# Flamingo cross-attention block with a long convolution: half-size transforms on half-reversed tokens, and a searched instruction order

## The chip, the cores and the metric

The kernel runs on one core of one Trainium2 chip. The metric is the device time of one launch in microseconds (us), from three runs of the kernel; a profiled execution, taken separately, gives the trace. Five engines with strict in-order queues share the work: PE (TensorE, matmuls), DVE (VectorE), ACT (ScalarE), POOL (GpSimd) and SP (SyncE, which issues most DMAs).

## The reference

The input is `x` of 8 batches x 512 tokens x 256 channels and a context of 8 x 1024 x 192, all float32. Per batch:

```
Q = ln(x) @ Wq ; K = ctx @ Wk                 # 4 heads of 32
scores = Q K^T / sqrt(32) ; keep the 32 largest of 1024 per row ; softmax over them
c = mean over heads of (probs @ ctx) @ Wv
h = ln(ln(x)) * (1 + g*scale_in(c)) + g*shift_in(c)
y = causal convolution of h along the 512 tokens with a kernel K[256, 512] + h * D_skip
y = y * (1 + g*scale_out(c)) + g*shift_out(c)
t = ln(x) + y ; t = t + gelu(ln(t) @ W1 + b1) @ W2 + b2
x = x + tanh(g1) * ln(t)
x = x + tanh(g2) * (shared_swiglu(ln(x)) + the one of 8 expert swiglus that the gate picks)
```

The convolution's kernel is computed on the chip from the state-space parameters (`A`, `C`, `log_dt`), once.

## The kernel before, in words

**Tiles.** Tokens lie on the 128 partitions, in NT = 4 blocks of 128 per batch; channels (256) lie along the free dimension. Everything is float32; a float32 matmul leaves two records in the trace.

**Stages of a batch.** `prepare` loads `xt` and `cx`, normalises, transposes (`pc`, `px`) and makes `kT`, `qT` (`pk`, `pq`). `attention` makes the scores of two heads at a time in `scores`: four 32-row matmuls `pS` into two PSUM banks (tag `sc`), which ACT copies to `sc` and DVE reads once more in `mn`; DVE's MAX8 and MATCH_REPLACE8 then find the 32nd largest value; ACT exponentiates; POOL adds the heads into `acc`; `weighted` transposes `acc` (`pa`) and multiplies it with the context (`pu`). `mixed` modulates (`film`: `pfi`, then `pfo`) and convolves. `after_mix` is the MLP (`hT`, `pm`, `am`), two layer norms, the gate, the scatter of the tokens by expert into the DRAM table `xtab`, and the shared expert (`p1`, `p2`, shown as `p`, and `ae`). `block` and `routed` gather 128 tokens of one expert from `xtab` (`xb`, `pxb`), load that expert's three weight matrices of 512 KB (`rt_gate`, `rt_up`, `rt_down`) and run it (`pg`, `pu`, `pyr`), then scatter-add into the output.

**The convolution before.** The 512 tokens are two halves of L = 256 (the axis `b` of 2 in the rearrangements), each of NL = 2 blocks `c` of 128. `spectrum` multiplies both halves at once (512 columns) with cosine and sine tables `ftab`: two groups of 128 frequencies `f`, real and imaginary part `r`, two blocks `c`, so 8 matmuls of 128x512 into `pxf`. DVE and POOL multiply with the kernel's spectra `kf` (`yf`, `t2`, `t3`). The way back is 8 more, `py`, two outputs of four terms.

**The order of the work.** The program first writes down every operation (class `Plan`) with its inputs, its outputs, a planned cost (`time`) and a priority `k`: the place at which it was written down, less a lead (`LEAD_A`, `LEAD_P`, `LEAD_S`). `order` then walks through a model of the five engines, the pools and the DMA wire: at each step, of the operations that could begin first, it takes the one with the smallest `k` (on ACT, one that needs another activation table counts as 100 later). The order so found is issued, and each engine executes its own part strictly in it. All operations are issued from line 323, `o.fn()`, so the profile's rows tell them apart by tile names. The order of batches is fixed: attention of batch b runs beside `mixed` and `after_mix` of batch b-1 and the routed blocks of batch b-2; 15 routed blocks are left for the end.

Of the kernel before, what the change touches and what calls it, by code (L numbers as in the profile page):

```python
# [22 lines left out]
P = 128  # L23
# [17 lines left out]

HOP = {"PE": 0.28, "DVE": 0.15, "ACT": 0.22, "POOL": 0.18, "SP": 0.1, "DMA": 0.1}
# [3 lines left out]
class Op:  # L46
    __slots__ = ("i", "eng", "fn", "cost", "lat", "table", "acc", "succ", "npred", "est", "tiles", "end", "start", "what", "k")


class Plan:  # L50
    def __init__(self, nc):
        self.nc = nc
        self.ops = []
        self.noting = False
        self.lead = 0
        self.seen = {}
        self.tiles = {}
        self.queues = {}
# [78 lines left out]
    def time(self, eng, method, out, outs, ins, args, kw, n):  # L137
# [7 lines left out]
        if eng == "DVE":  # L145
            width = max([n] + [self.width(v) for v in ins])
            if method in ("max", "match_replace", "tensor_reduce", "bn_stats", "bn_aggr", "reciprocal", "max_index"):
                t = 0.065 + 0.0012 * width
                if method in ("match_replace", "max_index"):
                    t += 0.08  # L150
            elif method in ("tensor_scalar", "tensor_copy", "memset"):
                t = (0.09 + 0.00115 * width) if psum else (0.30 + 0.0006 * width)
            elif len(outs) > 1:
                t = 0.25 + 0.00133 * width
            else:
                t = 0.07 + 0.0012 * width + (0.0 if psum else 0.1 + 0.0008 * width)
            return t, None
        if eng == "ACT":
            t = max(0.24, 0.085 + 0.00104 * n) + (0.19 if len(outs) > 1 else 0)
            if not psum and 128 < n <= 256:  # L160
                t += 0.16
            f = args[2] if method == "activation" else None
            return t, (TABLES.get(str(f).split(".")[-1]) if f is not None else None)
        if eng == "POOL":
            if kw.get("op") == ALU.pow or (len(args) > 3 and args[3] == ALU.pow):
                return 1.05, None
            if method in ("memset", "iota"):
                return 0.3 + 0.0005 * n, None
            if method in ("tensor_scalar", "tensor_copy"):
                return 0.23 + 0.002 * n, None  # L170
            return 0.17 + (0.0028 if out.dtype == I32 and method == "tensor_tensor" and args[3] == ALU.add else 0.0022) * n, None
# [9 lines left out]
    def add(self, op, ins, outs, whole=False):  # L181
        op.i = len(self.ops)
        op.k = op.i - self.lead
# [36 lines left out]
    def order(self):  # L220

        ops = self.ops
        free = {e: 0.0 for e in ("PE", "DVE", "ACT", "POOL", "SP")}
        table = None
        wire = 0.0
        left = {t: len(v[1]) for t, v in self.tiles.items()}
        last = {t: 0.0 for t in self.tiles}
        slots = {}
        for q in self.queues.values():
            slots[id(q)] = [0.0] * q[0]  # L230
        granted = set()
        avail = {e: [] for e in free}
        done = []

        def offer(op):
            op.npred -= 1
            if op.npred == 0:
                avail[op.eng].append(op)

        for op in ops:  # L240
            op.npred += 1 + len(op.tiles)

        def grant(q):
            s = slots[id(q)]
            while s and q[2] < len(q[1]):
                t = q[1][q[2]]
                q[2] += 1
                at = min(s)
                s.remove(at)
                for i in self.tiles[t][1]:  # L250
                    ops[i].est = max(ops[i].est, at)
                    offer(ops[i])

        for q in self.queues.values():
            grant(q)
        for op in ops:
            offer(op)
        total = len(ops)
        while len(done) < total:
            best = None  # L260
            for e, a in avail.items():
                if not a:
                    continue
                t = free[e]
                first = min(max(t, o.est) for o in a)
                c = None
                for o in a:
                    if o.est <= first:
                        k = o.k + (SWITCH if e == "ACT" and o.table not in (None, table) else 0)
                        if c is None or k < c[0]:  # L270
                            c = (k, o)
                o = c[1]
                st = max(t, o.est)
                if best is None or (st, o.k) < best[0]:
                    best = ((st, o.k), o, st)
            assert best is not None, "nothing can begin"
            _, o, st = best
            e = o.eng
            avail[e].remove(o)
            cost = o.cost  # L280
            if e == "ACT" and o.table not in (None, table):
                cost += 1.3
                table = o.table
            o.start = st
            free[e] = o.end = st + cost
            done.append(o)
            if o.lat is not None:
                wire = max(o.end, wire) + (o.lat - 2.9 if o.lat > 2.9 else 0.0)
                fin = max(o.end + o.lat, wire + 2.9)
                o.end = fin  # L290
            else:
                fin = o.end
            for i in o.succ:
                s = ops[i]
                hop = HOP["DMA" if o.lat is not None else e] if (s.eng != e or o.lat is not None) else 0.0
                s.est = max(s.est, fin + hop)
                offer(s)
            for t in o.tiles:
                left[t] -= 1
                last[t] = max(last[t], fin)  # L300
                if left[t] == 0:
                    q = self.tiles[t][0]
                    slots[id(q)].append(last[t] + 0.15)
                    grant(q)
        self.total = max(o.end for o in ops)
        self.free = free
        return done

    def ahead(self, gen, lead):
        while True:  # L310
            self.lead = lead
            end = next(gen, StopIteration) is StopIteration
            self.lead = 0
# [12 lines left out]
SLOW = 1.05  # L326
# [17 lines left out]
def tile_kernel(ctx: ExitStack, tc: tile.TileContext, a: dict, out: bass.AP):  # L344
# [10 lines left out]
    ND, NH, NIC, NF = D // P, HID // P, NI // P, T // P  # L355

# [45 lines left out]
    def accs(name):  # L402
# [14 lines left out]
                     base=0, channel_multiplier=-1)  # L417
    plan.noting = True
# [12 lines left out]
    def prepare(b, s):  # L431
# [46 lines left out]
        for c in range(ND):  # L478
            p_ = bank(f"px{b}_{c}")
            for t in range(NT):  # L480
                TE.transpose(p_[:, t * P : (t + 1) * P], s.xt[:, t, c * P : (c + 1) * P], ident)
            S.copy(xT[:, c, :], p_)
        yield
        s.qT = pk.tile([P, T], F32, tag="qT", name=f"qT{b}")
# [20 lines left out]
    for b, s_ in enumerate(states):  # L505
        s_.prep = plan.ahead(prepare(b, s_), LEAD_P)
# [15 lines left out]
    ftab = const.tile([P, 3, NL, L], F32, name="ftab")  # L522
# [58 lines left out]
    def transposed(src, tag, name, g=None, b=None):  # L581

        t_ = pr.tile([P, ND, T], F32, tag=tag, name=name)
        for c in range(ND):
            p_ = bank(f"{name}_p{c}")
            for t in range(NT):
                TE.transpose(p_[:, t * P : (t + 1) * P], src[:, t, c * P : (c + 1) * P], ident)
# [5 lines left out]

    def spectrum(src, f, r, name):

        p_ = bank(name)
        blocks = src.rearrange("p (b c) d -> p c b d", b=2)
        for c in range(NL):
            TE.matmul(p_, ftab[:, r, c, f * P : (f + 1) * P], blocks[:, c],
                      start=(c == 0), stop=(c == NL - 1))  # L600
        return p_.rearrange("p (b d) -> p b d", b=2)


    def setup():
# [179 lines left out]
        q.dma_start(gin[:, 1], row(a["L0_xattn_b_norm_in"], DK + 1))  # L784
        ft = a["ftab"].rearrange("(c p two) r f -> p two r c f", p=P, two=2)
        for i, r in enumerate((0, 1, 1)):
            SY.dma_start(ftab[:, i], ft[:, 0, r, :NL, :L])
        altc = a["alt"].rearrange("(p o) -> p o", o=1)
        altr = a["alt"].rearrange("(o p) -> o p", o=1)
        for c in range(NL):  # L790
            SY.dma_start(ftab[:, 1, c, 0:1], altc)
# [690 lines left out]
```

## Time and profile before

| | us |
|---|---|
| median of 3 runs | 1792.97 (1792.47 to 1794.63) |
| profiled execution | 1794.11 |
| its span (first to last instruction) | 1792.3 |
| busy PE | 1513.1 (84%) |
| busy DVE | 1302.1 (73%) |
| busy ACT | 1154.6 (64%) |
| busy POOL | 931.5 (52%) |
| mean granted PE clock | 0.874 of full speed |

"Busy" is time in which an engine executes at least one instruction. A row of a group reads: line, engine, operation, output tile<-input tiles, shapes, number of records; then busy time, mean of one record in ns; then the time that the engine had stood idle just before them, and what ended it. Matmul records overlap, so their mean is longer than their share of the time.

### The profile page before, as it was taken

The page shows a single profiled execution, that of the slowest core. Times are in us where ns is not written, and L with a number is a line of the kernel's source. Part 1 is how long each engine was busy: PE and PEld are TensorE (multiplying, and loading weights), DVE is VectorE, ACT ScalarE, POOL GpSimd, SP SyncE. Part 2 cuts the span into 40 slices and gives each one's busy share as a digit, 9 for nine tenths or more (in the row PEclk, how much of TensorE's full clock was granted, in tenths as well). Part 3 has the DMA queues.
Part 4 walks back from the last instruction along what each step waited for, and adds up shares of the span by engine and source line. Part 5 has one row for each costly group of instructions (what it writes and reads, how often), then busy time and mean ns, then how long its engine had stood idle before and what let it go on. Part 6 is the DMA issues. An engine that isn't in the chain of part 4 may idle for free. (4 is left out here: it accounts for less than half of the span.)

```text
span 1792.3 us, 21191 instructions
## 1 busy us (share of the span) xinstructions
PE 1513.1 (84%) x6363; PEld 893.1 (50%) x6363; DVE 1302.1 (73%) x3073; ACT 1154.6 (64%) x2008; POOL 931.5 (52%) x1072
## 2 busy tenths in 40 slices
PE   5365577797998798999889999998999989889885
PEld 2143333344543454465436554654465547547685
DVE  6989977885878697977798889697978987222210
ACT  4778844676747774887578877885788678123121
POOL 5578544445363645465555765474557646233122
PEclk8555677786998799998989999998999989989898
DMA  4000110001200120143103330431033205523794
GB/s 118 0 1 24 33 35 18 12 12 47 70 20 12 47 65 18 36 128 96 54 12 109 91 102 12 135 107 58 12 111 107 66 12 162 179 103 86 228 280 117
DMA packets 101289, 131.68 MB, mean 73 GB/s; under 512 B 9687, under 2 KB 73004, under 8 KB 101166
## 3 DMA queue, kind: packets, MB, share of 16 engines
q1 hardware_dynamic: 93102, 121.05, 21.1%
q0 software_dynamic: 7008, 8.42, 2.6%
q8 instruction: 52, 0.85, 0.2%
q10 hardware_dynamic: 1056, 0.79, 0.1%
q14 instruction: 71, 0.58, 0.1%
HBM read 112.22 MB, written 18.78 MB: 73 GB/s over the span
## 5 line engine op out<-in xcount | busy, mean ns | idle before, releaser
L323 PE MATMUL pS<-kT,qT 32*128 32x512 f32 x512 | 285.6, 742 | 71.2 <-DVE mn L323 61.0
L323 POOL TENSOR_TENSOR acc<-acc,e 128x1024 f32<-128x1024 f32 x96 | 229.0, 2385 | 182.3 <-ACT e L323 179.9
L323 DVE MAX8 top<-mn 128x8 f32<-128x256 f32 (+1 forms) x512 | 276.0, 556 | 11.9
L323 ACT COPY sc<-pS 128x512 f32<-128x512 f32 x256 | 145.6, 584 | 167.1 <-PE pS L323 136.9
L323 DVE SCALAR_TENSOR_TENSOR e<-sc,t,e 128x1024 f32<-128x1024 f32 x128 | 180.3, 1421 | 40.6 <-ACT e L323 40.3
L323 DVE TENSOR_TENSOR mn<-sc,pS 128x512 f32<-128x512 f32 x256 | 165.2, 677 | 35.9 <-PE pS L323 19.9
L323 POOL TENSOR_TENSOR mn<-mn 128x256 int32<-128x256 int32 x128 | 102.4, 800 | 164.4 <-DVE hi L323 163.8
L323 PEld LDWEIGHTS pS<-kT,qT 32*128 32x128 f32 x512 | 75.9, 208 | 203.6 <-DVE mn L323 98.9
L323 ACT ACTIVATE e<-sc,sm 128x1024 f32<-128x1024 f32 x128 | 145.1, 1146 | 16.1 <-POOL acc L323 13.2
L323 ACT ACT_TABLE_LOAD x118 | 151.4, 1283 | 4.0 <-issue 2.0
L323 PE MATMUL pm<-hT,w 128*128 128x512 f32 x256 | 137.9, 677 | 13.6 <-ACT hT L323 13.6
L323 ACT ACTIVATE junk<-sc,sm 128x1024 bf16<-128x1024 f32 x128 | 146.1, 1141 | 1.3
L323 PEld LDWEIGHTS pu<-aT,cx 128*96 128x96 f32 x1024 | 122.2, 168 | 28.6 <-issue 24.1
L323 PE MATMUL pu<-aT,cx 128*96 128x128 f32 x1024 | 135.4, 282 | 0.2 <-ACT aT L323 0.2
L323 PE MATMUL am<-w,ga 128*128 128x256 f32 x512 | 129.1, 398 | 6.1 <-ACT ga L323 6.1
L323 PEld LDWEIGHTS am<-w,ga 128*128 128x128 f32 x512 | 96.9, 196 | 51.4 <-issue 27.6
L323 POOL DMA_INDIRECT out_dram<-yb,to x38 | 61.5, 1620 | 96.7 <-DMA out_dram<-yb,to 46.3
L323 ACT ACTIVATE e<-e,sm 128x1024 f32<-128x1024 f32 x96 | 108.5, 1147 | 1.6 <-DVE sm L323 1.6
L323 POOL TENSOR_TENSOR mn<-mn,hi 128x256 int32<-128x256 int32 x128 | 104.9, 819 | 8.0
L323 DVE TENSOR_TENSOR ger<-sgr,pu 128x512 f32<-128x512 f32 x38 | 26.0, 684 | 108.7 <-PE pu L323 105.9
L323 DVE MATCH_REPLACE8 mn<-top,mn 128x256 f32<-128x256 f32 x256 | 104.6, 409 | 0.0
L323 POOL TENSOR_TENSOR yf<-yf,t 128x512 f32<-128x512 f32 (+1 forms) x80 | 85.2, 1089 | 35.0 <-DVE t L323 33.7
(287 smaller groups left out, 3125.0 us busy)
## 6 DMA issues: line engine op xcount, KB each, us to landing
rt_gate<-in_L_ffn_rt_gate_dram SPq DMA_DIRECT2D x38, 512.0 KB
rt_up<-in_L_ffn_rt_up_dram SPq DMA_DIRECT2D x38, 512.0 KB
rt_down<-in_L_ffn_rt_down_dram SPq DMA_DIRECT2D x38, 512.0 KB
w<-in_L_xattn_W_dram SPq DMA_DIRECT2D x32, 512.0 KB
cx<-in_ctx_dram SPq DMA_DIRECT2D x7, 768.0 KB
xtab<-zt SPq DMA_DIRECT2D x8, 642.5 KB
xb<-xtab SPq DMA_DIRECT2D x38, 128.5 KB
xt<-in_x_dram SPq DMA_DIRECT2D x8, 512.0 KB
```

The lines of the kernel that those rows point to most:

```text
L323: o.fn()
```

## The change

Four things change together.

1. *Tokens.* Of each pair of 128-token blocks (t = 0,1 and t = 2,3), the odd block is kept in reverse order from `prepare` to `after_mix`. `anti` is the exchange matrix. Odd blocks are transposed with it instead of `ident`, so that `qT` is in reverse order and `hT` back in natural order. A matmul with `anti` turns the odd blocks of `xt` (and two columns of statistics) into reverse order; ACT copies them back. In the MLP two matmuls with `anti` add the odd blocks of `xr` in natural order into the accumulators `am`, so that ACT only copies these out.
2. *Transforms.* With tokens n and 255-n of a half on the same partition, frequencies of even and odd number need only their sum or only their difference. DVE makes the difference `df` and, in place, the sum; each of four spectra is then one matmul instead of two. Back, the even and the odd part (`pyu`, `pyw`) are two outputs of two terms each, and their sum and difference are the two blocks. The frequencies of a group are now all even or all odd; the tables are cut in set-up from `ktab` and `htab`.
3. *Planned costs.* The formulas of `time` have other constants (`SLOW` 1.05 becomes 1.12).
4. *The order.* `walk` is the same model as before, written with heaps. `order` tries 220 sets of shifts of the priorities, by kind of work (attention, preparation, scores, routed blocks, the rest) and sixteenth of the program, and keeps the set with the shortest sum of two walks in which every cost is drawn up to 20% longer.

```diff
-                    t = 0.065 + 0.0012 * width
+                    t = 0.15 + 0.00104 * width
...
+    def order(self):
+        self.compile()
+        rng = random.Random(1)
+        ops = self.ops
+        part = [(o.kind, o.i * PARTS // len(ops)) for o in ops]
+        longer = [[o.cost * (1.0 + SPREAD * rng.random()) for o in ops] for _ in range(2)]
+        def tried(shift):
+            _, done = self.walk([o.k - shift[p] for o, p in zip(ops, part)])
+            return sum(self.walk(order=done, cost=c)[0] for c in longer), done
+        shift = dict.fromkeys(part, 0)
+        parts = list(shift)
+        best, order = tried(shift)
+        for _ in range(WALKS):
+            new = dict(shift)
+            for p in rng.sample(parts, rng.choice((1, 2, 4, 8))):
+                new[p] += rng.choice((-1, 1)) * rng.choice((10, 30, 80, 200))
+            t, o = tried(new)
+            if t <= best:
+                best, order, shift = t, o, new
...
-SLOW = 1.05
+WALKS, PARTS, SPREAD = 220, 16, 0.2
+SLOW = 1.12
...
+    turn = (ident, anti)
...
-                TE.transpose(p_[:, t * P : (t + 1) * P], s.xt[:, t, c * P : (c + 1) * P], ident)
+                TE.transpose(p_[:, t * P : (t + 1) * P], s.xt[:, t, c * P : (c + 1) * P], turn[t % 2])
...
+        for v, n in ((s.xt, D), (s.rs2.unsqueeze(2), 1)):
+            p_ = bank(f"pr{b}_{n}")[:, : 2 * n].rearrange("p (b d) -> p b d", b=2)
+            x1 = v.rearrange("p (b c) d -> p c b d", c=2)[:, 1]
+            TE.matmul(p_, anti, x1, start=True, stop=True)
+            S.copy(x1, p_)
...
+        xs, xd = (xm.rearrange("p (b c) d -> p c b d", c=2)[:, k] for k in range(2))
+        df = pk.tile([P, 2, D], F32, tag="sg", name=f"df{b}")
+        V.tensor_sub(df, xs, xd)
+        V.tensor_add(xs, xs, xd)
...
-            re, im = (spectrum(xm, f, r, f"pxf{b}_{f}_{r}") for r in range(2))
+            re, im = bank(f"pxf{b}_{f}_0"), bank(f"pxf{b}_{f}_1")
+            for r, p_ in enumerate((re, im)):
+                TE.matmul(p_, ftab[:, r, f], xs if f == r else df, start=True, stop=True)
...
-        for c in range(NL):
-            p_ = bank(f"py{b}_{c}")
-            steps = [(f, r) for f in range(NL) for r in range(2)]
-            for i, (f, r) in enumerate(steps):
-                TE.matmul(p_, ftab[:, 2 * r, f, c * P : (c + 1) * P], yf[:, f, r].rearrange("p b d -> p (b d)"),
-                          start=(i == 0), stop=(i == len(steps) - 1))
...
+        pu, pw = bank(f"pyu{b}"), bank(f"pyw{b}")
+        for p_, k in ((pu, 0), (pw, 1)):
+            for f in range(NL):
+                r = f if k == 0 else 1 - f
+                TE.matmul(p_, itab[:, f, r], yf[:, f, r].rearrange("p b d -> p (b d)"),
+                          start=(f == 0), stop=(f == NL - 1))
+        x0, x1 = (xr.rearrange("p (b c) d -> p c b d", c=2)[:, k] for k in range(2))
+        pw3 = pw.rearrange("p (b d) -> p b d", b=2)
+        S.copy(x0, pu.rearrange("p (b d) -> p b d", b=2))
+        V.tensor_sub(x1, x0, pw3)
+        V.tensor_add(x0, x0, pw3)
...
+            if k == 0:
+                for t in range(1, NT, 2):
+                    TE.matmul(acc[t // 2][:, 1, :], anti, xr[:, t, :], start=False, stop=False,
+                              skip_group_check=True)
...
-            V.tensor_add(xr[:, 2 * i : 2 * i + 2], xr[:, 2 * i : 2 * i + 2], acc[i])
+            V.tensor_add(xr[:, 2 * i], xr[:, 2 * i], acc[i][:, 0])
+            S.copy(xr[:, 2 * i + 1], acc[i][:, 1])
```

## The prediction

> **What bounds the kernel now.** I read first the busy time by stretch. The stretches end where the last score matmul of batch 0 ends (233.6 us), where that of batch 7 ends (1484.3), where the last attention sums are reduced (1550.5) and where the last scatter of tokens has landed (1680.6). Columns: length, then busy us and instructions of PE, weight loads, DVE, ACT, POOL, then granted clock, DMA share, GB/s.
>
> ```profile
> 0.00:233.60 233.60, 125.73 (x757) 71.44 (x757) 197.01 (x336) 170.15 (x288) 151.75 (x142) 0.61 0.15 40
> 233.60:1484.30 1250.70, 1126.77 (x4178) 622.17 (x4177) 1024.74 (x2519) 889.84 (x1549) 676.67 (x797) 0.91 0.18 56
> 1484.30:1550.50 66.20, 62.56 (x368) 49.26 (x368) 33.96 (x97) 43.78 (x73) 41.29 (x58) 1.00 0.55 174
> 1550.50:1680.60 130.10, 109.38 (x433) 69.54 (x432) 35.88 (x106) 30.59 (x53) 35.34 (x47) 0.93 0.41 137
> 1680.60:1792.30 111.70, 88.61 (x632) 80.69 (x632) 10.48 (x16) 20.24 (x45) 26.50 (x30) 0.91 0.69 201
> ```
>
> The start is DVE's (84% busy, clock 0.61 on PE). The main stage, 1250.7 us for seven batches, is PE's: 90% busy, DVE 82%. The last stretch is weight traffic of the routed blocks at 201 GB/s. Next I read the groups of instructions by shape, for prices (busy us, mean ns of one record, idle before).
>
> ```profile
> L323 PE MATMUL pS<-kT,qT 32*128 32x512 f32 x512 | 285.6, 742 | 71.2 <-DVE mn L323 61.0 <-ACT sc L323 8.9 <-DMA rt_gate<-in_L_ffn_rt_gate_dram 1.1
> L323 PE MATMUL am<-w,ga 128*128 128x256 f32 x512 | 129.1, 398 | 6.1 <-ACT ga L323 6.1
> L323 PE MATMUL py<-yf,ftab 128*128 128x512 f32 x128 | 58.8, 600 | 0.7 <-POOL yf L323 0.7
> L323 PE MATMUL pxf<-xm,ftab 128*128 128x512 f32 x128 | 58.8, 600 | 0.0
> L323 DVE TENSOR_TENSOR ta<-ta,tk 128x512 f32<-128x512 f32 x8 | 12.9, 1616 | 0.2
> L323 DVE TENSOR_TENSOR xr<-xr,am 128x512 f32<-128x512 f32 x16 | 10.2, 680 | 38.5 <-PE am L323 38.5
> L323 DVE TENSOR_TENSOR tk<-tk,ta 128x512 f32<-128x512 f32 x8 | 9.0, 1126 | 6.2 <-POOL ta L323 6.0
> ```
>
> Each f32 matmul leaves two records and they overlap, so I divide busy time by half the count: 58.8/64 = 0.92 us for a 128x512 one, 129.1/256 = 0.50 for 128x256, 285.6/256 = 1.12 for a score matmul. Then PE's timeline, for the score matmuls, and PE's waits in the main stage:
>
> ```profile
> 1461.06 1.12 PE L323 MATMUL pS<-kT,qT 32*128 32x512 f32 x2
> 1462.11 1.56 PE L323 MATMUL am<-w,ga 128*128 128x256 f32 x6
> 1463.60 1.13 PE L323 MATMUL pS<-kT,qT 32*128 32x512 f32 x4
> ```
>
> ```profile
> PE pc L323 <- DMA cx<-in_ctx_dram: 25.6, 5, 6.0
> PE pS L323 <- DVE mn L323: 24.8, 14, 7.7
> ```
>
> One score matmul alone (2 records) takes 1.12 us; two of different heads next to each other (4 records) take 1.13 together. A neighbour saves about 1.05 us of PE. The waits are short and scattered.
>
> **The change, part by part.**
>
> *Transforms.* Per batch 8 forward and 8 inverse 128x512 matmuls become 4 and 4: half of 58.8+58.8, so -58.8 us. Added on PE per batch: one 128x512 matmul that turns `xt` (8 x 0.92 = 7.4), two 128x256 that turn `xr` into the accumulators (16 x 0.50 = 8.1), and a two-column one (about 0.1 each, as the 128x16 `pz` with 27.2 us for 256; 0.8). Net -42.5 us, 5.3 a batch. The transposes with `anti` replace ones with `ident` at the same shape: nothing.
>
> *DVE.* Per batch the difference and sum of two SBUF halves are new: 16 of 128x512. Nearest rows: `tk`, 1.13 us, and `ta`, 1.62 us. I take 1.13, 18 us. Two new 128x512 ones with a PSUM operand: 16 x 0.68 = 10.9. Two 128x512 adds of `am` shrink to 128x256 (0.42 by the `xr<-xr,pfo` rows): -4.2. Sum +25 us, 3.1 a batch. Here a rule speaks against the change: the Trainium skill, "SBUF — State Buffer", section "SBUF: two separate sides", says that a DVE operation with two SBUF inputs and a GpSimd one that reads SBUF exclude each other for the whole instruction. POOL's commonest add lasts 2.39 us; if each of the 16 stood behind one, DVE would lose 38 us more. The gap between the two rows, 0.49 us, would make 8. I take 0, and keep 38 for the range.
>
> *ACT.* One `xr` copy fewer, one `xt` copy more, a tiny one (0.2) and two 128x256 copies (0.37) more a batch: +7.5; nine table loads fewer in the built order (109 against 118, 1.28 each): -11.5. Set-up adds three copies and trades three table transfers for four. About 0, and hidden: ACT is 71% busy in the main stage.
>
> *The order.* Planner prices, priorities and 220 passes decide only the order on the engines, so I counted both built orders. (1) Neighbouring score pairs of different heads, batches 1 to 7: 36 before, 57 after: 21 x 1.05 = -22 us of PE. (2) PE work behind the last score matmul, each family at its row's price: 301 becomes 271; the rows' sum exceeds the busy time by 1.09, so 27 us, of which 5 are the last batch's transforms. So 22 us of PE (the end of batch 6's MLP, two routed blocks' matmuls of batch 5) and about 9 of DVE (two layer norms of batch 6) move into the main stage.
>
> *Main stage.* PE: -37 (7 x 5.3) + 22 - 22 = -37. DVE: +22 + 9 = +31. If PE alone set it, with its 124 us of waits unchanged: 1214, -37. If DVE alone did: +31. PE is nearer to its limit, and DVE waits for it (41.6 us for `pfi`, 19.9 for `pS`), so I pass on two thirds: -24. The second rule weighed is the Trainium skill's "TensorE: Matmul & The Clock Gate", Part 1: after an idle window of about 3.4 us PE runs at half clock. The trace shows it in the tail, after a wait of 4.0 us: 16 gate matmuls take 3.61 us where others take 1.95.
>
> ```profile
> 1558.78 0.44 PE L323 MATMUL pxb<-ident,xb 128*128 128x128 f32 x2 [4.00 <-DMA xb<-xtab]
> 1559.68 3.61 PE L323 MATMUL pg<-xbT,rt_gate 128*128 128x128 f32 x16 [0.46 <-ACT xbT L323]
> 1563.13 1.95 PE L323 MATMUL pu<-xbT,rt_up 128*128 128x128 f32 x16
> 1564.91 1.88 PE L323 MATMUL pfi<-wf,uT 97*128 97x512 f32 x4
> ```
>
> By the rule, 37 freed us gathered in seven gaps of 5 would give back 7 x 1.7 = 12 and leave -12; by the rows, freed time spread over short waits costs nothing. The work leaves in pieces of 1 to 4 us, so I keep -24.
>
> *Tail.* From the last score matmul to the transposes of the last attention sums (1544.6) passed 60 us, PE full. POOL's last add was done at 1528.7, so 16 us of that were PE's backlog. The new order takes 22 off PE and two layer norms off DVE there, but puts three of batch 6's scatters (some 3.7 us apart) ahead of the last add: -18. Then the last `pfi` stood behind a whole routed block until 1564.9; now behind one of its eight gate matmuls: of 10.1 us since the previous `pfi`, the 4.0 of waiting for `xb` and 1 stay, -5; difference and sum cost 2 x 1.13 on this path: -3 together. Halved transforms (-2 here), the new adds (+1) and the turned `xr` in the MLP (+1) cancel. The 13 blocks at the end keep their order: 0. Tail -21.
>
> *Start.* Three table loads fewer, DVE 2 us less before the last score matmul of batch 0: -2.
>
> Sum -24 - 21 - 2 = -47. The profiled execution took 1794.1 us (span 1792.3 and 1.8 around it), so 1747; the median of the runs is 1.1 lower: **1746 us**.
>
> **The rivals.**
> - *The search does more.* It also halves PE's waits for `cx` (25.6), for `hd` (15.1) and for `xm` (7.8), 24 us, and the whole 37 pass: -61 -23, 1709. For it: the new prices are nearer to the rows (a 256-wide MAX8 0.42, row 0.43). Against: score matmuls stay priced at half of what one alone takes.
> - *The main stage gives nothing*, DVE's 31 us eating PE's 37: -23, 1770.
> - *DVE sets the main stage*: +31 - 21 - 2 = +8, 1801. For it: the start is DVE's already; against: 18% idle in the main stage.
> - *Pairs that wait.* A pair needs both score banks free, and PE, strictly in order, holds everything behind it until DVE has read both. Waits of `pS` for `mn` average 1.8 us, the longest 7.7. Were the 21 new pairs to wait 4 us more each, +84 - 37 - 21 - 2 = +24, 1817. It decides from 60/21 = 2.9 us each.
>
> **How the numbers follow.** The likeliest case, 0.55, reaches from 1725 (all 37 pass, one wait trimmed) to 1768. Search does more 0.12; nothing in the main stage 0.15; DVE 0.10; pairs 0.08. Faster by over 0.2% (3.6 us, about what a measurement can tell) 0.82, slower 0.16, between 0.02. The range from 1715 to 1797 leaves out some 0.05 below and 0.15 above; the extra 38 us of DVE would lie in that part.
>
> **What would show it.** Right: `pxf`, and the inverse's groups together, at 29.4 us each; more rows of four score records at 1.13; main stage PE busy near 1090; the wait before the last `pfi` gone. Wrong: `df` rows above 1.6 us, `pS` waits for `mn` grown by 60 us, or a DVE share near 90% between batches.

## The result, and the profile after

The changed kernel takes **1823.01 us** (median, 1820.01 to 1828.47), the kernel before beside it 1793.72 us. The ratio is 1.0171, with a 95% interval of 1.0146 to 1.0196: slower by 31 us, where 47 us of gain were predicted (1793 to 1746). The profiled execution has a span of 1822.3 us (before 1792.3) at a mean granted PE clock of 0.852 (before 0.874).

Busy time by stretch, changed kernel, cut at the same events as in the prediction, save that the two last stretches are one here (columns: length, busy us and instructions of PE, weight loads, DVE, ACT, POOL, then granted clock, DMA share, GB/s):

```profile
0.00:237.02 237.02, 130.87 (x763) 74.03 (x763) 199.01 (x347) 167.91 (x290) 154.00 (x147) 0.60 0.13 35
237.02:1527.40 1290.38, 1115.22 (x4251) 629.43 (x4250) 1051.86 (x2560) 904.66 (x1590) 701.47 (x807) 0.89 0.19 58
1527.40:1822.30 294.90, 242.07 (x1289) 185.07 (x1287) 75.51 (x200) 76.78 (x148) 92.86 (x122) 0.90 0.53 165
```

The start is 3 us longer, the tail 13 us shorter (308.0 became 294.9), and the main stage 40 us longer: 1250.7 became 1290.4. PE has 12 us *less* to do in the main stage than before, and stands idle 175 us in it instead of 124.

The groups of the changed kernel that answer to those shown of before (busy us, mean ns of one record, idle before and what ended it):

```profile
L366 PE MATMUL pS<-kT,qT 32*128 32x512 f32 x512 | 268.2, 733 | 89.5 <-DVE mn L366 57.5 <-ACT sc L366 31.9
L366 PE MATMUL pyu<-yf,itab 128*128 128x512 f32 x32 | 21.7, 768 | 9.8 <-POOL yf L366 9.8
L366 PE MATMUL pyw<-yf,itab 128*128 128x512 f32 x32 | 21.3, 759 | 12.4 <-POOL yf L366 12.0 <-DVE t L366 0.3
L366 PE MATMUL pxf<-xm,ftab 128*128 128x512 f32 x32 | 16.8, 606 | 1.9 <-DVE t L366 1.2 <-DVE xm L366 0.7
L366 PE MATMUL pxf<-df,ftab 128*128 128x512 f32 x32 | 16.4, 599 | 0.0
L366 PE MATMUL am<-xr,anti 128*128 128x256 f32 x32 | 9.2, 414 | 0.0
L366 PE MATMUL pr<-xt,anti 128*128 128x512 f32 x16 | 9.2, 658 | 0.0
L366 DVE TENSOR_TENSOR df<-xm 128x512 f32<-128x512 f32 x8 | 5.5, 691 | 0.3
L366 DVE TENSOR_TENSOR xm<-xm 128x512 f32<-128x512 f32 x8 | 9.6, 1202 | 0.3
```

The matmuls were halved as foreseen, 128 records each way becoming 64, but they were not halved in time: the inverse (`pyu` and `pyw`) is 43.0 us where 29.4 were expected. And there are waits that did not exist: `pyu` and `pyw` stand 22 us for POOL's `yf`, where `py` had stood 0.7.

The sum (`xm<-xm`) has a mean of 1202 ns, but that is a mean of two kinds: six of the eight took 0.69 us, like the difference, and two took 2.73. DVE in batches 2 and 3, and POOL beside the second of them (no POOL operation overlaps the first):

```profile
681.46 0.69 DVE L366 TENSOR_TENSOR xm<-xm 128x512 f32<-128x512 f32 x1
...
868.77 2.73 DVE L366 TENSOR_TENSOR xm<-xm 128x512 f32<-128x512 f32 x1
...
868.21 5.51 POOL L366 TENSOR_TENSOR acc<-acc,e 128x1024 f32<-128x1024 f32 x2 [14.80 <-ACT e L366]
```

The first of those two POOL additions ended at 870.94, and the sum 0.56 us later. The other long sum, in batch 0, ended 0.56 us after a POOL addition too.

PE's waits in the main stage (sum, times, longest), changed kernel:

```profile
PE hT_p L366 <- ACT hh L366: 31.2, 7, 5.8
PE pS L366 <- DVE mn L366: 30.7, 11, 10.9
PE pc L366 <- DMA cx<-in_ctx_dram: 29.9, 6, 5.9
PE pS L366 <- ACT sc L366: 22.0, 11, 10.0
PE pyw L366 <- POOL yf L366: 10.3, 4, 3.5
PE pyu L366 <- POOL yf L366: 9.8, 2, 5.4
```

and, of the kernel before, the two of them that the prediction did not show:

```profile
PE hT_p L323 <- ACT hh L323: 13.9, 6, 3.8
...
PE pS L323 <- ACT sc L323: 4.8, 5, 2.3
```

So the transposes ahead of the MLP (`hT`) wait 17 us more, the score matmuls 17 us more for ACT, the inverse 20 us more. Other waits fell: that of `hdT` for `hd` from 15.1 to 3.9 us, that of `pm` for `hT` from 12.9 to 4.5. What the waits of the inverse look like in one batch is in PE's timeline. Before, batch 2 (start, length, instruction, records; a wait is in brackets):

```profile
679.17 4.32 PE L323 MATMUL pfi<-wf,uT 96*128 96x512 f32 x6
683.33 0.38 PE L323 MATMUL pc<-ident,cx 128*96 128x128 f32 x2
683.55 4.46 PE L323 MATMUL pxf<-xm,ftab 128*128 128x512 f32 x10
687.93 1.12 PE L323 MATMUL pS<-kT,qT 32*128 32x512 f32 x2
688.99 1.13 PE L323 MATMUL pxf<-xm,ftab 128*128 128x512 f32 x2
689.95 1.02 PE L323 MATMUL pfo<-wf,uT 97*128 97x512 f32 x2
690.90 1.12 PE L323 MATMUL pS<-kT,qT 32*128 32x512 f32 x2
691.95 1.98 PE L323 MATMUL pxf<-xm,ftab 128*128 128x512 f32 x4
...
694.92 2.85 PE L323 MATMUL pfo<-wf,uT 96*128 96x512 f32 x6
...
698.90 1.88 PE L323 MATMUL py<-yf,ftab 128*128 128x512 f32 x4
```

and changed:

```profile
679.56 2.74 PE L366 MATMUL pfo<-wf,uT 97*128 97x512 f32 x6
682.14 1.02 PE L366 MATMUL pxf<-df,ftab 128*128 128x512 f32 x2
...
687.00 1.10 PE L366 MATMUL pxf<-xm,ftab 128*128 128x512 f32 x2 [0.93 <-DVE t L366]
692.48 2.07 PE L366 MATMUL pyu<-yf,itab 128*128 128x512 f32 x2 [4.39 <-POOL yf L366]
694.35 1.91 PE L366 MATMUL pyw<-yf,itab 128*128 128x512 f32 x2
```

Before, the long forward transform, the matmuls of the films `pfo` and some score matmuls fill the time in which DVE and POOL make the products, and the first inverse matmul `py` finds them done: PE has no pause. Changed, the planner has moved three of the films' matmuls (6 records) *ahead* of the forward transform, where they fill the time of the new sum and difference on DVE. Behind the short transform too little is left, PE waits 4.39 us for POOL, and the two matmuls after the wait take 2.07 and 1.91 us (granted clock 0.50 in that stretch) where the same shape took 1.02 us a moment before.

### The profile page after: what moved, and what is told of

Same layout as the page of the kernel before. It is cut to its first block, busy times and chain, and to the rows that moved or that the text cites. A ratio compares the mean times of both kernels' runs of the same rounds, so it can differ in the third digit from the quotient of the medians.

```text
span 1822.3 us, 21150 instructions
## 1 busy us (share of the span) xinstructions
PE 1488.2 (82%) x6299; PEld 888.5 (49%) x6299; DVE 1326.4 (73%) x3105; ACT 1149.4 (63%) x2026; POOL 948.3 (52%) x1074
## 5 line engine op out<-in xcount | busy, mean ns | idle before, releaser
L366 PE MATMUL pS<-kT,qT 32*128 32x512 f32 x512 | 268.2, 733 | 89.5 <-DVE mn L366 57.5
L366 POOL TENSOR_TENSOR acc<-acc,e 128x1024 f32<-128x1024 f32 x96 | 232.9, 2426 | 154.5 <-ACT e L366 146.9
L366 ACT COPY sc<-pS 128x512 f32<-128x512 f32 x256 | 144.1, 585 | 141.0 <-PE pS L366 116.7
L366 DVE SCALAR_TENSOR_TENSOR e<-sc,t,e 128x1024 f32<-128x1024 f32 x128 | 187.8, 1480 | 29.9 <-ACT e L366 29.0
L366 PEld LDWEIGHTS pS<-kT,qT 32*128 32x128 f32 x512 | 70.7, 205 | 211.6 <-DVE mn L366 90.8
L366 POOL TENSOR_TENSOR yf<-yf,t 128x512 f32<-128x512 f32 (+1 forms) x80 | 90.8, 1159 | 71.7 <-DVE t L366 70.4
```

## The experiments

Differences are worked out from the ratios, each to the runs of the kernel before on the same chip: (ratio - 1) x 1794 us. On that scale the changed kernel is at +31. "Order held" means that the planned order on every engine is that of the kernel named, and only what an operation issues is exchanged, by a helper of this kind:

```diff
+    def also(self, *fns):
+        fns = (self.ops[-1].fn,) + fns
+        self.ops[-1].fn = lambda: [f() for f in fns]
+    def instead(self, fn=lambda: None):
+        self.ops[-1].fn = fn
```

**Which of the change's parts loses.** Four kernels split it: the new transforms on the old planner (`t_only`), the new planner without them (`order_only`), the new prices alone (`costs_only`: the diff is that of `order_only` with `WALKS` at 0), and transforms and prices without the passes (`t_costs`).

```diff
 t_only:      every hunk from "anti = const.tile" on; time(), order(), SLOW as before
 order_only:  time(), SLOW, walk(), order() as changed; mixed(), after_mix(), prepare() as before
-WALKS, PARTS, SPREAD = 220, 16, 0.2
+WALKS, PARTS, SPREAD = 0, 16, 0.2        # costs_only, t_costs
```

> The halved transforms and the reversed tokens with the planner of before (old costs, one greedy walk, no search). Theory 'order': the searched order lost the time and the transforms gain what was costed, 5.3 us of PE a batch, so 1745 to 1780 us. Theory 'transforms': the shorter matmuls leave the chain from the sum and difference over DVE and POOL to the layer norm uncovered, so the transforms alone lose, 1805 to 1840 us, with PE waiting for yf and hh as in the changed kernel.

> The transforms of before with the new costs and the 220 passes. Theory 'order': 1800 to 1840 us, slower than before by itself. Theory 'transforms': no slower than before, 1750 to 1795 us.

> The transforms of before, the new planned costs, no pass of the search. If the new prices alone misplace work, this is slower than before by 15 us or more; if the passes do it, within 10 us of before while the run with the 220 passes is slower.

> The changed kernel without its 220 passes: new transforms, new costs, the first walk. If the passes lose the time, 1750 to 1790 us. If the transforms lose it, 1810 us or more; then the passes helped or did nothing.

| | median us | ratio (95%) | against before |
|---|---|---|---|
| t_only | 1866.22 | 1.0395 (1.0357 to 1.0432) | +71 |
| order_only | 1805.43 | 1.0071 (1.0040 to 1.0102) | +13 |
| costs_only | 1814.95 | 1.0113 (1.0081 to 1.0145) | +20 |
| t_costs | 1854.96 | 1.0334 (1.0300 to 1.0368) | +60 |

The theory that the order alone lost the time falls: transforms and reversal lose 71 us on the old planner, and with them the 220 passes win 29 (60 to 31). Without them the passes win 7, which is within the noise, and the new prices lose 20, so a new plan by itself can move this kernel by 20 us. The new planner is no gain without the transforms: +13. A second seed of the search asks whether the loss is the luck of one order:

```diff
-        rng = random.Random(1)
+        rng = random.Random(2)
```

> The changed kernel with another seed of its search of 220 passes, nothing else: another order of about the same planned length. If the 1823 is the transforms' price under any order: within 10 us of it, 1813 to 1833. If it is one order's luck: further off, either way, 1790 to 1850.

Measured: 1820.94 us, ratio 1.0122 (1.0087 to 1.0158), +22; the profiled one had a span of 1828.8. The loss is there in another order too.

**Is PE's work what counts, or the chain through the other engines?** In the trace of before the first `pfi` of a batch begins 0.1 to 5.8 us after the last `ae` of the batch before, so the operations of `mixed` and `after_mix` follow each other with little slack. Four kernels in held orders; all but `b_link` leave something out. `a_unlink` also leaves out the reversing matmuls in the MLP and all but a column of the sum behind the inverse.

```diff
+            if t == NT - 1:                                     # b_link, after the last write of xm
+                plan.also(partial(nc.vector.tensor_sub, xs, xs, xd), partial(nc.vector.tensor_add, xs, xs, xd))
...
+                    if g % 2:                                   # b_lesspu, in weighted
+                        plan.instead()
...
         V.tensor_sub(df, xs, xd)                                # a_nosum
+        plan.instead(partial(nc.vector.tensor_sub, df[:, 0, 0:1], xs[:, 0, 0:1], xd[:, 0, 0:1]))
...
         V.tensor_sub(x1, x0, pw3)                               # a_unlink, besides
+        plan.instead(partial(nc.vector.tensor_copy, x1, pw3))
```

> The kernel before, its planned order held, with two VectorE operations of 128x512 put between the last write of xm and the first forward matmul of every batch (xm's even blocks minus the odd, then plus the odd again: the value is the same but for rounding). PE gets nothing to do. Theory 'chain' (the main stage is paced by the serial chain of behind(b), in which the first pfi of a batch starts as the last ae of the batch before ends): in the changed kernels this link lengthened pfi to pxf from 2 to 29 us over 7 batches, so +20 to +30: 1813 to 1823 us. Theory 'load' (the stage is paced by the sum of PE's work, as the prediction read it): PE has 113 us of idle time there to take 8 pauses of 2 to 4 us, so 0 to +6: 1793 to 1799 us.

> The kernel before, its planned order held, with half of the attention's weighted sums pu left out (the odd of the eight groups of keys: the attention output is wrong by that; 512 of 1024 matmul records of 135.4 us, so 67.7 us less of PE, none of it in behind(b)). Theory 'load': two thirds of the 59 us that lie in the main stage, and some in the setup stage: -40 to -55, so 1739 to 1754 us. Theory 'chain': attention is 20 to 35 us ahead of the chain already, so only what chain matmuls queue behind pu is won: 0 to -20, so 1774 to 1794 us.

> The changed kernel, its planned order held, with the sum and the difference ahead of the halved forward transform cut from 128x512 to one column each and the difference's matmuls fed with the odd blocks (the sums are left out, so the convolution is wrong). PE's work is the same. Theory 'chain': pfi to pxf goes from 29 us over 7 batches back to some 5, and 3 in the last batch: -20 to -30, 1793 to 1803 us. Theory 'load': VectorE has 15 us less to do, which PE does not wait for: 0 to -5, 1818 to 1823 us.

> As a_nosum, and besides: x1 becomes a copy of pw's bank that does not wait for x0, the sum into x0 is cut to a column, and the 16 matmuls with the reversing table in the MLP are left out (9.2 us of PE); the convolution and the residual are wrong by these. Theory 'chain': on top of the 20 to 30 us of the sums, 10 to 20 of the 17 to 22 by which py to hT grew, and 9 to 15 of the MLP's growth: -40 to -60, 1763 to 1783 us. Theory 'load': two thirds of 9.2 us and the 0 to 5 of the sums: -6 to -11, 1812 to 1817 us.

Measured: b_link 1821.83 us, 1.0143 (1.0113 to 1.0174), +26. b_lesspu 1784.13, 0.9946 (0.9927 to 0.9966), -10. a_nosum 1828.15, 1.0212 (1.0157 to 1.0266), +38, the profiled one 1820.6 in span. a_unlink 1820.40, 1.0136 (1.0101 to 1.0172), +24.

On the kernel before, the chain's theory hits twice: 16 operations on DVE, an engine 73% busy, cost 26 us, and 58 us of PE's records that vanish (`pu` 135.4 to 76.9) win only 10. On the changed kernel it misses twice: taking the same link out gives nothing. The timeline of `a_nosum` says why: in the held order the films still stand between `pfi` and `pxf` (in batch 2 the same 6 records, 2.74 us), so `pxf` comes no earlier, and `pyu` waits 4.38 us as in the changed kernel. Whether the link costs anything could only be seen with the order free, below.

**Which piece of the transforms?** On the old planner, forward and inverse were put back to the form of before, one at a time and together.

```diff
-                TE.matmul(p_, ftab[:, r, f], xs if f == r else df, start=True, stop=True)    # t_inv, t_rev
+                for c, x_ in enumerate((xs, xd)):
+                    TE.matmul(p_, ftab[:, r, f], x_, start=(c == 0), stop=(c == NL - 1))
...
-        pu, pw = bank(f"pyu{b}"), bank(f"pyw{b}")                                            # t_fwd, t_rev
+        for c in range(NL):
+            p_ = bank(f"py{b}_{c}")   # four matmuls, one copy, two films, as before
```

> The transforms alone, on the planner of before, with the inverse put back to the form of before: per half four full matmuls, one copy, two films, the second half's matmuls beside the first half's films (the tables are the halved ones, so the numbers that come out are wrong). Forward halved, reversal kept. Beside it stand the kernel before at 1794 and the whole transforms at 1866 on this planner. Theory 'inverse': of the 1866 the most came with PE's idle time between the inverse's first matmul and the MLP's first transpose (17 us before, 51 us with the transforms, batches 1 to 6): -35 to -50, so 1816 to 1831 us. Theory 'forward' (the sum and difference ahead of it, as the link put into the kernel before cost 28 us): no gain, PE has 38 us more: 1855 to 1885. Theory 'luck' (re-planning scatters by 20 us and that is all): 1774 to 1814.

> The mirror of it: the inverse halved, reversal kept, and the forward transform as before, eight matmuls a batch and no sum or difference (wrong numbers again). Theory 'inverse': the wait between inverse and MLP stays and 42 us of PE come back, in stretches where PE is needed: 1855 to 1885 us. Theory 'forward': without the link -28 or more: 1825 to 1845 us. Theory 'luck': 1774 to 1814.

> Both transforms in the form of before, so that only the reversal of the odd blocks is left of the change: pr in prepare, the reversing table in the transposes, the 16 reversing matmuls in the MLP and the ACT copies in place of half of the adds (wrong numbers). Its parts are 21 us of PE, 11 us of ACT and -3 us of VectorE. Theories 'inverse' and 'forward' alike: two thirds of 21 us, +5 to +20: 1799 to 1814 us. If reversal is where the time went: 1840 or more.

| | median us | ratio (95%) | against before |
|---|---|---|---|
| t_rev: reversal only | 1830.70 | 1.0213 (1.0187 to 1.0239) | +38 |
| t_inv: and inverse halved | 1838.59 | 1.0247 (1.0217 to 1.0277) | +44 |
| t_fwd: and forward halved | 1851.88 | 1.0325 (1.0297 to 1.0353) | +58 |
| t_only: both | 1866.22 | 1.0395 (1.0357 to 1.0432) | +71 |

Neither theory had this: half of the loss is the reversal, and halving makes every kernel here slower, forward (with its sums) by 20 and inverse by 6 when each is halved alone, with less on PE (busy 1547.4, 1531.5 and 1525.8). In t_rev PE's busy time grew by 34.3 us and the span by 34.6; 23 us of it are the reversal's own matmuls and 13 the score matmuls, which stood less often in pairs in that order (`pS` 298.9 against 285.6). PE's time and the span grew alike in that plan, but one such pair does not show that the one made the other. Each of these is a new plan, with the 20 us of scatter that costs_only shows, so the split is rough.

**What the pauses cost.** Matmuls that do nothing were put where PE waits, in the order of the changed kernel and in that of before.

```diff
+            w = ftab.rearrange("p a b c -> p (a b c)")[:, :512]
+            plan.ops[-1].fn = lambda: [nc.tensor.matmul(p_, anti, w, start=True, stop=True) for _ in range(n)] + [f()]
...
+                    fill(p_, 2 if k == 0 else 1)      # ahead of pyu, pyw
+                    fill(p_, 4)                       # ahead of hT's first transpose
```

> The changed kernel, its planned order held, with matmuls of 128x512 that do nothing put on PE where it waits: 2 ahead of the first matmul of pyu, 1 ahead of the first of pyw, 4 ahead of the first transpose of hT (56 in all, each overwritten by the work that follows; some 0.9 us each). PE waited there 22 and 36 us. If the pauses cost twice, because the matmuls after them run at half clock (hT_p 448 ns in the changed kernel against 364 before, pyu 768 against 600): -8 to -20, 1803 to 1815 us. If they cost only themselves: 0 to +12, 1823 to 1835 us, as part of the fillers runs over.

> The kernel before, its planned order held, with matmuls of 128x512 that do nothing ahead of the first transpose of hT (3) and of hdT (2) in every batch, where PE waited 20 and 16 us in all. If half clock after a pause costs there too (hT_p 364 ns, px 304): -2 to -8, 1786 to 1792 us. If pauses cost only themselves: +2 to +8, as 40 fillers are 39 us against 36 of waits.

Measured: a_warm 1814.09 us, 1.0107 (1.0072 to 1.0142), +19, so 12 us *faster* than the changed kernel, give or take 8 by the two intervals, although PE is busy 40 us longer (1527.9 against 1488.2); the clock rose from 0.852 to 0.867. b_warm 1793.79, 0.9992 (0.9975 to 1.0008): no difference, with PE 33 us busier (the profiled execution was one of its longest, 1804.29). The same place in a_warm, PE's timeline:

```profile
692.89 1.88 PE L1130 MATMUL pyu<-ftab,anti 128*128 128x512 f32 x4
697.45 2.07 PE L1130 MATMUL pyu<-yf,itab 128*128 128x512 f32 x2 [2.68 <-POOL yf L366]
699.31 1.52 PE L1130 MATMUL pyw<-ftab,anti 128*128 128x512 f32 x2
700.67 1.02 PE L1130 MATMUL pyw<-yf,itab 128*128 128x512 f32 x2
```

The first and the third line are fillers. `pyu` still comes after a pause (2.68 us) at half speed here (granted clock 0.50), `pyw` no longer. In the changed kernel `pyu` and `pyw` had a mean record of 768 and 759 ns; with the fillers the four groups of them lie between 638 and 680.

**What the removed matmuls are worth, and what the added ones cost.** a_double puts the halved work back, b_load adds the reversal's matmuls to the order of before.

```diff
                 TE.matmul(p_, itab[:, f, r], y_, start=(f == 0), stop=(f == NL - 1))     # a_double; pxf alike
+                plan.also(partial(nc.tensor.matmul, p_, zero, y_, start=False, stop=(f == NL - 1)))
...
+                    plan.also(partial(nc.tensor.matmul, acc[t // 2][:, 1, :], zero, xr[:, t, :], ...))   # b_load
```

> The changed kernel, its planned order held, with each of the transforms' halved matmuls followed by one of the same shape with zero weights into the same bank (the result is the same): the PE work that the halving took out is back, 60 to 75 us of records, with everything else of the change as it is. Theory 'load' (as predicted: two thirds of PE's microseconds pass into the time): +40 to +50, 1863 to 1873 us. Theory 'cover' (they lay beside the chain yf, xr, hh through POOL, VectorE and ACT, and PE waits out what is not filled, at half clock after it): -5 to +12, 1818 to 1835 us.

> The kernel before, its planned order held, with the reversal's matmuls alone added, as matmuls that change nothing: two records of 128x512 and two of two columns ahead of pq in every batch, and four of 128x256 with zero weights after the first MLP step (21 us of PE in the profile of the reversal alone, which was 37 us slower than before). If a PE microsecond costs itself where PE has no wait: +14 to +21, 1808 to 1815 us, and the rest of the 37 belongs to what else the reversal does (ACT's copies, 10 more table loads, and an order in which the score matmuls stand less in pairs: pS 13 us more). If the reversal's matmuls cost more than themselves: +30 or more. If PE has room: 0 to +7.

Measured: a_double 1842.33 us, 1.0250 (1.0218 to 1.0282), +45, so 14 over the changed kernel for 65.2 us of added records. PE's busy time rose by only 38 (1526.4), because the rows of neighbouring groups overlap and so count some time twice, and because the inverse's own records became shorter (768 to 609 ns: 43.0 to 33.7 us). Counted once, the records of all transforms grew by 45 us, from 71.6 to 116.7. The wait of `pyw` went from 12 to 0.1 us. b_load 1805.01, 1.0056 (1.0040 to 1.0071), +10, for 21.7 us of records. So the saving that the change is made for is worth 14 us where it lies (some 7 us either way), and both results lie between their theories.

**With the order free.** Sums and reversal were taken out one at a time and the rest planned by the same search.

```diff
-        V.tensor_sub(df, xs, xd)                                       # a_nosum_plan
-        V.tensor_add(xs, xs, xd)
...
-    turn = (ident, anti)                                               # a_norev_plan
+    turn = (ident, ident)
-            TE.matmul(p_, anti, x1, start=True, stop=True)
-                    TE.matmul(acc[t // 2][:, 1, :], anti, xr[:, t, :], start=False, stop=False, ...)
...                       # the copies out of pr and am go too; DVE adds am as before
```

> The changed kernel without the sum and the difference ahead of the forward transform (the matmuls read the even and the odd blocks as they are, so the convolution is wrong), planned afresh by the same search. If the link is a cause that the fixed order hid, the 20 to 28 us that it cost elsewhere come back: 1795 to 1803 us. If the search had already placed work into the gap at no cost: 1813 to 1828 us.

> The changed kernel without the reversal of the odd blocks (no pr, plain transposes, no reversing matmuls in the MLP, VectorE's add in place of the ACT copies; wrong numbers), planned afresh by the same search. By b_load the matmuls alone are worth 10 us, by the reversal alone on the old planner all of it 37: -10 to -37, 1786 to 1813 us. If reversal costs nothing in this order: 1815 to 1828 us.

Measured: a_nosum_plan 1807.41 us, 1.0067 (1.0045 to 1.0089), +12; a_norev_plan 1793.31, 0.9999 (0.9987 to 1.0012), 0. The first falls between its theories, the second within its range. Without the sums the planner laid the films back between and behind the forward matmuls; PE's timeline of a_nosum_plan in batch 2:

```profile
680.51 1.56 PE L366 MATMUL pxf<-xm,ftab 128*128 128x512 f32 x2
681.91 1.02 PE L366 MATMUL pfo<-wf,uT 97*128 97x512 f32 x2
682.77 1.02 PE L366 MATMUL pxf<-xm,ftab 128*128 128x512 f32 x2
...
687.93 0.93 PE L366 MATMUL pc<-ident,cx 128*96 128x128 f32 x7
689.19 1.10 PE L366 MATMUL pyu<-yf,itab 128*128 128x512 f32 x2 [0.33 <-ACT cT L366]
690.12 1.02 PE L366 MATMUL pyw<-yf,itab 128*128 128x512 f32 x2
```

Hardly a pause before `pyu` (0.33 us), and full speed. The waits of the inverse for POOL fell from 21.8 to 9.8 us over the whole kernel. PE's waits in the whole of a_norev_plan, by contrast:

```profile
PE hT_p L366 <- ACT hh L366: 30.8, 8, 6.0
PE pS L366 <- ACT sc L366: 30.4, 19, 7.1
PE pyu L366 <- POOL yf L366: 11.0, 4, 5.4
```

The changed kernel has 36.3, 31.9 and 9.8 there (and 12.0 for `pyw`), the kernel before 19.0, 8.9 and 0. So the longer waits for `hh` and `sc` stand also in a kernel that loses nothing: with 37 us less on PE (busy 1476.3) and 34 more of waiting it takes as long as before. They can account for the gain that is missing, not for the 31 us on top, which come with the reversal.

Where the time goes is seen if each batch is cut at its own operations on PE. Sums over batches 1 to 6, in us, from the traces (the step from the last `ae` to the next `pfi`, 5 to 15 us in all, is left out):

| | first to last `pfi` | to first `pxf` | to first inverse matmul | to first `hT` | to last `ae` |
|---|---|---|---|---|---|
| before | 163 | 0 | 94 | 131 | 668 |
| changed | 183 | 22 | 64 | 154 | 661 |
| a_nosum_plan | 172 | 1 | 72 | 142 | 679 |
| a_norev_plan | 168 | 24 | 67 | 141 | 667 |
| t_rev | 182 | -1 | 94 | 132 | 680 |

From before to changed, the transforms give back 30 us; what follows them up to `hT` (22 more) and the sums ahead of them (22) take more than that. The reversal is seen in the films `pfi`: 15 us from a_norev_plan to the changed kernel, 19 from before to t_rev. Why it would lengthen them no run shows, and a_nosum_plan, which has the reversal, is only 4 over a_norev_plan there.

## Why the prediction was wrong

**The parts, one at a time.** The changed kernel stands at +31. Halving, as a_double measures it, is worth -14; the sums cost 31 - 12 = 19, the reversal 31 - 0 = 31, and the new planner by itself 13. Together +49, 18 too many: the parts are not independent of each other, and each one with a free order carries the 20 us by which a new plan can move this kernel. Only the reversal stands clear of that, and it costs about the same on both planners (31 and 38). The prediction had halving at two thirds of -58.8, the sums at nothing in the main stage, the reversal's matmuls at two thirds of 16.3, and the new order as a gain.

**The step that failed** is the one under *Main stage*: "If PE alone set it, with its 124 us of waits unchanged: 1214, -37 ... so I pass on two thirds: -24". Measured +40. A PE 90% busy was read as the bound, and a microsecond of PE as worth the same wherever it lies. Two more terms failed with it: the reversal was priced by its matmuls alone (two thirds of 16.3 us; it cost 31), and the sums ahead of the forward transform only as part of DVE's total, at nothing in the chain (they cost 19, or 26 for such a pair in the kernel before). In a held order PE's microseconds were worth:

| kernel, order held | rows of PE records added | PE busy | time |
|---|---|---|---|
| b_lesspu: off the chain, far ahead of need | -58.5 | -38 | -10 |
| a_double: in the transforms, beside POOL and DVE | +65.2 | +38 | +14 |
| b_load: in `prepare` and the MLP, where PE hardly waits | +21.7 | +17 | +10 |
| a_warm: in pauses, changed kernel | +58.5 | +40 | -12 |
| b_warm: in pauses, kernel before | +42.6 | +33 | 0 |

By the rows, in which the prediction counted, at no place two thirds pass (by busy time b_load comes near, 10 of 17). The waits were not unchanged either: the work that was taken away had been the cover of a chain through DVE, POOL and ACT (products, `yf`, films, statistics, `hh`), and PE's idle time in the main stage rose by 51 us while its busy time fell by 12.

Point by point:

- *Transforms on PE*: the count was right, the size not. -58.8 was forecast, -41.4 is what the rows show (117.6 to 76.2); of the missing 17 us 14 are in the inverse, whose matmuls follow a pause. Added matmuls: 21.3 us against 16.3.
- *Clock*: the rule of the Trainium skill, "TensorE: Matmul & The Clock Gate", Part 1, would have turned seven gaps into 12 us, and was set aside because the work "leaves in pieces of 1 to 4 us". The work did, but the waits came in one piece: 4.39 us ahead of `pyu` in the batch shown, up to 5.8 ahead of `hT`. Filling them won 12 us. That this is the rule's number says little: a_warm also made the waits themselves shorter, so the two are not separated. Half speed came earlier than by the rule, after pauses of 2.2 to 2.3 us in t_costs, t_fwd and t_inv, and in a_unlink not after one of 3.46. The kernel before gained nothing from fillers, though two of the pauses they filled, at `hdT`, were 7.5 us long (those at `hT` at most 3.8 in the main stage). The "16 gate matmuls" of the prediction are 16 records, so eight matmuls.
- *DVE*: +25 forecast, +24.3 measured (1302.1 to 1326.4); `df` and the sum took 0.69 us each when nothing stood beside them, against 1.13. That DVE and POOL shut each other out, which the prediction had weighed, fits two of the 16: sums of 2.73 us that ended just after a POOL addition. That is 4 of the 38 us, so taking 0 was nearly right in size. They stand between `pfi` and `pxf`, and of what hides them, the films, nothing was said. Left out and planned anew they gave back 19 us, which by itself is within the scatter of new plans; a pair of the same kind in the kernel before, its order held, cost 26. Only in the tail was the sum put on the path.
- *ACT*: 0 forecast, 1154.6 to 1149.4 measured: right as a total. The reversal's copies were called hidden, and its 31 us are three times what its matmuls cost alone (b_load, 10). The rest, 20 us, stays open: the copies out of `am` and `pr`, the table loads and the order were not separated.
- *Order*: pairs of score matmuls were counted right (-22 forecast, 285.6 to 268.2 measured, -17), and so was the tail's backlog: from the last score matmul to the transposes of the last attention sums 60 us became 39 (42 forecast). The last `pfi` came 2 us sooner after them, not 5: the wait for `xb` ahead of it grew from 4.0 to 6.3 us instead of staying. It then took 3.62 us instead of 1.88, and all from its start on 10 us longer, which was not foreseen: tail -13 for -21. By itself the new planner costs 13.
- *Start*: -2 forecast, +3 measured.
- *Rivals*: the number lies nearest to "pairs that wait" (1817), whose mechanism is not what happened: the waits of `pS` for `mn` grew by 6 us in the main stage, not by 84. That DVE sets the main stage is not it either: it stood idle 18% before and after. No rival had the cover, and none the reversal.

No version here that computes the whole block beats the kernel before. The best of the planned ones, a_norev_plan, equals it, and leaves the reversal out. Tokens that come in reverse order from memory would do without it; that was not tried.

## What to carry to other kernels

On an engine that is 90% busy, ask of each piece of work that goes away what waits behind it and on which other engine that is being made; if the next instruction waits for a chain through two other engines, the piece was cover, and its removal buys an idle engine and a slow clock. Book an added operation where it stands in the chain and name the work that hides it, because a planner that moves that work forward uncovers the place where it came from. Price a microsecond by adding or removing one in a held order before a rewrite: outside pauses that gave 0.2 to 0.5 us each here, where 0.67 had been assumed. A held order prices only what that order lets through, though: leaving the sums out gave nothing in the held order and 19 us in a new one.

## What the runs showed of the hardware that was not expected

- 56 matmuls of 128x512 with nothing to compute (58.5 us of records), put where PE waited, made a kernel 12 us faster (4 to 20).
- In all traces here, a 128x512 float32 matmul of the inverse (two records) that came behind a pause took 2.07 or 2.08 us after every pause over 3.5 us, and 1.10 to 1.13 after all but one of those of 0.9 to 1.6 us. In between both came: 2.08 after 2.21 us in t_costs, 1.13 after 3.46 us in a_unlink.
- Adding 65.2 us of matmul records raised PE's busy time by only 38 us, and leaving out 58.5 us lowered it by 38 as well. Rows of neighbouring groups overlap; in a_double the records behind pauses also became shorter, by 9 us.
- A subtraction and an addition of two SBUF halves on DVE (128x512 float32) took 0.69 us each, in place or not. Two of the 16 in the changed kernel met a POOL addition that had begun about 0.5 us before them, and took 2.73.
